# A state-space block on one core: one wait of VectorE for four exponentials made 8 units ahead, aggregates and scales a slot behind their sources, delta projections in two pairs

## The chip, the core and the metric

The kernel runs on one core of a Trainium2 chip. The metric is the device time of one execution in microseconds. The five engines of the core that matter are TensorE (PE: matmuls, and transposes as matmuls), VectorE (DVE), ScalarE (ACT), GpSimd (POOL) and SyncE (SP, which issues most of the DMAs). Each runs its own list of instructions in order; an instruction waits for semaphores that others raise, and everything behind it on its engine waits with it.

## What is computed

The input `x` is 8 sequences of 2048 tokens with 512 channels, float32. The block is a selective state-space layer (S6) with a residual, and then a feed-forward layer with quantized weights and a residual:

```python
u = layernorm(x)
xp = u @ x_proj_w.T                     # 512 -> 64 (rank) + 16 (B) + 16 (C)
delta = softplus(xp[..., :64] @ dt_proj_w.T + dt_proj_b)
h = exp(delta * A) * h + delta * B * u  # over time, for each channel and each of 16 states
y = (h * C).sum(states) + u * D
x = x + y
z = layernorm(x)                        # z quantized to int8 by row, times int8 weights
x = x + (round(z / s) @ weight_q.T) * s * weight_scale + bias
```

The recurrence over time is the heart: 16 states x 512 channels, each a scan along the sequence.

## The kernel before

**Tiling.** The sequence is cut into chunks of 512 tokens: four to a sequence, 32 in all. Within a chunk the recurrence is cut into 64 *units*: 16 states `n` times four groups `d` of 128 channels. A unit is one scan of VectorE over a tile of 128 channels x 512 tokens. The main loop takes one *slot* for each unit, so a chunk has slots 0 to 63, and unit u = 4n + d is scanned in slot u. The loop only writes instructions into the engines' lists; there is no barrier between slots, and each engine runs ahead as far as its waits and buffers allow. All instructions of the loop are pinned to the order in which they are written (`pin`), so the order written by hand is each engine's order.

**What a slot writes**, in this order (main loop, lines 552 to 573):

- in the first slot of a state: `c_mult` of the state before (GpSimd: the last column of h into `state[n]`, line 485, then h times C over all four groups at once, line 488), and every second state a load of two rows of C (SP, line 476)
- `exp_unit`, ScalarE, line 412: exp(delta x A) of a unit some places ahead, into a tile `da`. The counter `ahead` starts at 5; slots 28 to 31 make none, and slots 21, 23, 25 and 33 make two. There are 8 `da` buffers, each free again when its scan is done
- `bt_piece`, ScalarE, line 428: a quarter of B x delta x u of the state two ahead (`bT`). For states 1, 5, 9 and 13 this is one DMA instead (a diagonal of B, `dg`), so slots 28 to 31 have no such ScalarE work
- `b_pe`, TensorE: turns B x delta x u of the unit two ahead into channel-major order in one of three PSUM banks (`pb`; line 451 by four transposes, line 442 by products with the diagonal)
- `scan`, VectorE, line 460: h of the unit from `da`, `pb` and the state carried over. In the first chunk of a sequence the carried state is the constant 0
- `y_pe`, TensorE, line 513: adds h x C of the unit ten back into the output y (`hc` transposed back)
- then the steps that `todo` holds for this slot: pieces of `prep` (the first layer norm and the projections of the next chunk) and of `post` (residual, second layer norm and the feed-forward of the chunk before)

**The steps of `prep` and `post`.** Each list gives a slot to every step; where two share a slot, `post` comes first. In `prep`: the statistics of the input are taken one chunk earlier still, in slots 21 to 27 (`stats`: bn_stats and bn_aggr on VectorE, lines 148 and 149), the reciprocal root on GpSimd (`rstd_of`), normalization (line 173), transposes of the normalized input (14 to 21), the projection to 96 rows (`xp_pe`, slots 22 and 23), its copy (`xp_act`, slot 24, line 207), the transpose of B (`bt_pe`, 25; `bt_act`, 26, which also sends four small DMAs), then delta: `dt_pe` (27 to 30, TensorE, line 247) and `softplus` (28 to 31, ScalarE, line 257), one group of channels in each slot, and last delta x u: `dlt_pe` (TensorE, line 265) and `du` (VectorE, line 270), slots 38 to 45. Softplus and exp lie in different tables of ScalarE: a table load stands before the first softplus and before the first exponential after the last.

In `post`: loads of the input (`load`, slots 1 to 4, SP, line 297), `residual` (7, 8, 10, 12; VectorE, line 301), `stats` (14, 16, 18, 19), normalization (31 to 34; line 306, into z), `amax` (33, 34, 36, 37: a reduction and at once the scale `xs` from it, lines 324 and 330), the reciprocal of the scales (38), rounding (40 to 43), and for each of four token tiles transposes of z (`q_pe`), their copy to bf16 (`q_act`), the product with the weights (`o_pe`, line 371) and its scaling (`o_out`: VectorE, line 380; GpSimd adds the residual, line 384; SP stores, line 385). GpSimd adds the bias to the residual in slots 35, 39, 43 and 47 (line 317).

**One bank for all of these.** Every TensorE result of `prep` and `post` (`misc`) goes through one PSUM bank; each must be read before the next is written.

Of the kernel before, what the change touches and what calls it, by code (L numbers as in the profile page):

```python
# [17 lines left out]
P = 128  # L18
# [8 lines left out]
def kernel(  # L27
# [112 lines left out]
    cts, bcs = {}, {}  # L140
    mvs, nmrs, rstds, x1, zs, qts = {}, {}, {}, {}, {}, {}
    das, pbs, bts, hs, hcs, ys = {}, {}, {}, {}, {}, {}

    def stats(key, i, n, src):
        if i == 0:
            mvs[key] = small.tile([P, n, 2], F32, tag=f"mv{n}", name=f"mv_{key}")
        st = small.tile([P, 6], F32, tag="st", name=f"st_{key}_{i}")
        pin(nc.vector.bn_stats(st, src))  # L148
        pin(nc.vector.bn_aggr(mvs[key][:, i, :], st))
# [16 lines left out]
    def prep(k):  # L166
# [106 lines left out]
        for i in range(NT):  # L273

            steps.append((21 + 2 * i - SLOTS, lambda i=i: stats(key, i, NT, xn[k][:, i, :])))
            steps.append((5 + i, lambda i=i: norm(i)))
            steps.append((14 + 2 * i, lambda i=i: xnt_pe(i)))
            steps.append((15 + 2 * i, lambda i=i: xnt_act(i)))
            steps.append((22 + i // 2, lambda i=i: xp_pe(i)))
            steps.append((27 + i, lambda i=i: dt_pe(i)))  # L280
            steps.append((28 + i, lambda i=i: softplus(i)))
            steps.append((38 + 2 * i, lambda i=i: dlt_pe(i)))
            steps.append((39 + 2 * i, lambda i=i: du(i)))
        steps.append((27 - SLOTS, lambda: rstd_of(key, NT)))
        steps.append((24, xp_act))
        steps.append((25, bt_pe))
        steps.append((26, bt_act))
        return sorted(steps, key=lambda at: at[0])

    def post(k):  # L290
# [28 lines left out]
        def amax(i):  # L319
            if i == 0:  # L320
                st["am"] = small.tile([P, NT], F32, tag="am", name=f"am_{k}")
                st["xs"] = small.tile([P, NT], F32, tag="xs", name=f"xs_{k}")
            pin(
                nc.vector.tensor_reduce(
                    st["am"][:, i : i + 1], zs[i], AX.X, ALU.max, apply_absolute_value=True
                )
            )

            pin(
                nc.vector.tensor_scalar(  # L330
                    st["xs"][:, i : i + 1],
                    st["am"][:, i : i + 1],
                    Q_EPS,
                    1.0 / 127.0,
                    ALU.max,
                    ALU.mult,
                )
            )
# [49 lines left out]
        for i in range(NT):  # L388
            steps.append((1 + i, lambda i=i: load(i)))
            steps.append(((7, 8, 10, 12)[i], lambda i=i: residual(i)))  # L390
            steps.append(((14, 16, 18, 19)[i], lambda i=i: stats(key, i, NT, x1[k, i])))
            steps.append((31 + i, lambda i=i: norm(i)))
            steps.append(((33, 34, 36, 37)[i], lambda i=i: amax(i)))
            steps.append((35 + 4 * i, lambda i=i: add_bias(i)))
            steps.append((40 + i, lambda i=i: rnd(i)))
            steps.append(((46, 48, 52, 56)[i], lambda i=i: q_pe(i)))
            steps.append(((47, 49, 53, 57)[i], lambda i=i: q_act(i)))
            steps.append(((50, 54, 58, 60)[i], lambda i=i: o_pe(i)))
            steps.append(((51, 55, 59, 61)[i], lambda i=i: o_out(i)))
        steps.append((19, lambda: rstd_of(key, NT)))  # L400
        steps.append((38, scales))
# [4 lines left out]
    def exp_unit(u):  # L406
# [4 lines left out]
        t = work.tile([P, T], F32, tag="da", bufs=8, name=f"da_{k}_{n}_{d}")  # L411
        pin(nc.scalar.activation(t, delta[k][:, d, :], AF.Exp, scale=a_neg[:, d, n : n + 1]))  # L412
        das[u] = t
# [40 lines left out]
    def scan(u):  # L454
        s, d = divmod(u, ND)
        k, n = divmod(s, N)
        if d == 0:
            hs[s] = work.tile([P, ND, T], F32, tag="h", bufs=3, name=f"h_{k}_{n}")
        pin(
            nc.vector.tensor_tensor_scan(  # L460
                hs[s][:, d, :],
                das.pop(u),
# [5 lines left out]
        )  # L468

# [73 lines left out]
    ahead = 5  # L543
# [8 lines left out]
    for k in range(NCHUNK + 1):  # L552
        for slot in range(SLOTS):
# [6 lines left out]
            if slot < 28 or slot > 31:  # L560

                for _ in range(2 if slot in (21, 23, 25, 33) else 1):
# [59 lines left out]
```

## Time and profile before

The median of three runs is 3148.9 us (3147.22 to 3153.0).

| | |
|---|---|
| profiled execution, its own time | 3150.26 us |
| its span | 3148.5 us |
| VectorE busy | 2931.5 us, 93% |
| TensorE busy (matmuls) | 2864.0 us, 91% |
| GpSimd busy | 2798.1 us, 89% |
| ScalarE busy | 2795.1 us, 89% |
| scans (lines 460) | 2048, 1261 ns with a state and 1201 ns without |
| exponentials (line 412) | 2048, 715 ns |
| h x C (line 488) | 512, 4566 ns |
| DMA | 276.78 MB, 88 GB/s |
| granted TensorE clock | 0.989 |

A busy time is the sum of the instructions' lengths as recorded. On VectorE and ScalarE the next instruction starts some 0.08 to 0.1 us before the recorded end of the one before, so the distance from start to start is the better measure of what an instruction costs: ten scans that are recorded with 1.25 us each take 11.7 us. A wait is shown in brackets as the idle time before an instruction and the instruction that ended it. Where an instruction waits for several engines, all but one of its waits are instructions of their own ahead of it, which the views do not count as busy.

### The profile page before, as it was taken

To read this page: it belongs to the slowest core of one execution; us is meant where nothing else is said; L and a number is where in the kernel's file an instruction comes from. 1 tells how busy PE (TensorE), PEld (TensorE's weight loads), DVE (VectorE), ACT (ScalarE), POOL (GpSimd) and SP (SyncE) were. 2 spreads that over 40 slices of the span, in tenths; PEclk is the share of its full clock that TensorE was granted. 3 is DMA by queue.
4 is the path that set the end of the run, shared out by engine and by line. 5 is a ranking of instruction groups with operands and counts; after the bars stand their busy time and mean duration, and the time that the engine had idled before them with its cause. 6 is when DMAs were issued, how large, how long until landed. Compare 5 with 4: busy or idle time off the path is not lost.

```text
span 3148.5 us, 58120 instructions
## 1 busy us (share of the span) xinstructions
PE 2864.0 (91%) x22050; PEld 2465.4 (78%) x22144; DVE 2931.5 (93%) x3239; ACT 2795.1 (89%) x4482; POOL 2798.1 (89%) x1417
## 2 busy tenths in 40 slices
PE   5999999999999999999999999999999999999996
PEld 4877888777887778887878877878878788877784
DVE  4999999999999999999999999999999999999995
ACT  5998899988999989899888999988999889998883
POOL 2889899988999889999898998999999998998896
PEclk8999999999999999999999999999999999999997
DMA  4222323223223123332233232233232232322221
GB/s 122 89 59 91 102 88 101 79 70 103 94 95 102 55 89 101 98 98 86 64 95 102 88 101 60 86 98 98 98 95 62 89 101 88 101 81 70 87 88 41
DMA packets 182105, 276.78 MB, mean 88 GB/s; under 512 B 81152, under 2 KB 81664, under 8 KB 181824
## 3 DMA queue, kind: packets, MB, share of 16 engines
q1 hardware_dynamic: 177664, 269.80, 27.3%
q8 instruction: 175, 2.87, 0.4%
q10 hardware_dynamic: 4160, 3.25, 0.3%
q14 instruction: 106, 0.87, 0.1%
HBM read 236.03 MB, written 36.96 MB: 87 GB/s over the span
## 4 chain that ended last, share of the span: by engine, by line
PE 40%; ACT 23%; DVE 15%; POOL 11%; issue 9%; DMA 1%; SPq 0%; ACTq 0%; POOLq 0%; DVEq 0%
PE y L513 11%; DVE h L460 11%; PE pb L451 9%; ACT da L412 9%; POOL hc L488 8%; ACT bT L428 7%; PE pb L442 7%; PE y L501 4%; PE pdt L247 3%; PE po L371 2%; ACT z L348 2%; DVE st_a L148 1%; PE pz L354 1%; PE pxp L197 1%; PE pxn L185 1%
## 5 line engine op out<-in xcount | busy, mean ns | idle before, releaser
L488 POOL TENSOR_TENSOR hc<-h,c 128x2048 f32<-128x2048 f32 x512 | 2335.7, 4566 | 30.3 <-issue 12.7
L460 DVE TENSOR_TENSOR_SCAN h<-da,state,pb 128x512 f32<-128x512 f32 x1536 | 1864.8, 1261 | 52.6 <-PE pb L451 52.1
L412 ACT ACTIVATE da<-delta,a_neg 128x512 f32<-128x512 f32 x2048 | 1423.5, 715 | 32.1 <-DVE h L460 31.6
L513 PE MATMUL y<-ident,hc 128*128 128x128 f32 x8192 | 1231.2, 273 | 5.6 <-POOL hc L488 5.6
L428 ACT ACTIVATE bT<-x,BT 128x512 f32<-128x512 f32 x1536 | 1093.6, 712 | 4.8 <-DVE x L270 4.8
L451 PE MATMUL pb<-ident,bT 128*128 128x128 f32 x6144 | 957.5, 278 | 133.1 <-DVE h L460 109.4
L451 PEld LDWEIGHTS pb<-ident,bT 128*128 128x128 f32 x6144 | 700.7, 141 | 387.7 <-issue 136.7
L513 PEld LDWEIGHTS y<-ident,hc 128*128 128x128 f32 x8192 | 965.4, 142 | 6.2 <-POOL hc L488 6.2
L460 DVE TENSOR_TENSOR_SCAN h<-da,pb 128x512 f32<-128x512 f32 x512 | 591.8, 1201 | 28.2 <-PE pb L451 24.8
L442 PE MATMUL pb<-dg,x 128*128 128x128 f32 x4096 | 561.1, 280 | 40.2 <-DVE h L460 38.0
L442 PEld LDWEIGHTS pb<-dg,x 128*128 128x128 f32 x4096 | 500.6, 192 | 80.7 <-DVE h L460 72.3
L384 POOL TENSOR_TENSOR o<-o,x 128x512 f32<-128x512 f32 x128 | 164.5, 1285 | 52.2 <-DVE o L380 48.9
L247 PE MATMUL pdt<-xp,dtproj_sb 128*128 128x512 f32 x256 | 144.1, 645 | 48.6 <-ACT delta L257 40.8
L190 ACT COPY xnT<-pxn 128x512 f32<-128x512 f32 x128 | 73.6, 575 | 119.4 <-PE pxn L185 119.4
L257 ACT ACTIVATE delta<-pdt,dtb_sb 128x512 f32<-128x512 f32 x128 | 88.2, 689 | 96.1 <-PE pdt L247 95.7
L317 POOL TENSOR_TENSOR x<-x,bias_b 128x512 f32<-128x512 f32 x128 | 163.7, 1280 | 0.9 <-ACT z L306 0.9
L380 DVE SCALAR_TENSOR_TENSOR o<-po,xs,ws_b 128x512 f32<-128x512 f32 x128 | 94.5, 738 | 52.6 <-PE po L371 52.6
L485 POOL COPY state<-h 128x4 f32<-128x4 f32 x384 | 75.2, 196 | 75.8 <-DVE h L460 70.7
L501 PE MATMUL y<-diag_d,xnT 128*128 128x128 f32 x1024 | 137.8, 278 | 0.0
L371 PE MATMUL po<-wq_sb,qT 128*128 128x512 bf16 x418 | 129.6, 388 | 8.7 <-ACT qT L360 2.2
L501 PEld LDWEIGHTS y<-diag_d,xnT 128*128 128x128 f32 x1024 | 127.0, 195 | 0.0
L306 ACT ACTIVATE z<-x,nmr_f,rstd_f 128x512 f32<-128x512 f32 x128 | 102.2, 801 | 24.9 <-POOL nmr_f L160 24.9
(51 smaller groups left out, 1685.5 us busy)
## 6 DMA issues: line engine op xcount, KB each, us to landing
c<-bc SPq DMA_DIRECT2D x256, 512.0 KB, 4.0
x<-in_x_dram SPq DMA_DIRECT2D x32, 1024.0 KB, 7.5
dg<-dg SPq DMA_DIRECT2D x128, 256.0 KB, 4.1
x<-in_x_dram SPq DMA_DIRECT2D x128, 256.0 KB, 6.1
out_dram<-o SPq DMA_DIRECT2D x128, 256.0 KB, 2.0
dg<-zeros ACTq DMA_DIRECT2D x8, 256.0 KB, 3.1
dg<-BT SPq DMA_DIRECT2D x128, 2.0 KB, 3.2
bc<-xp SPq DMA_DIRECT2D x32, 32.0 KB, 1.6
```

The source lines that it names most:

```text
L247: nc.tensor.matmul(pd, lhsT=dtproj_sb[:, ts(d, P)], rhs=xp, start=True, stop=True)
L317: pin(nc.gpsimd.tensor_tensor(x1[k, i], x1[k, i], bias_b, ALU.add))
L371: nc.tensor.matmul(po, lhsT=qt[:, d, :], rhs=wq_sb[:, d, :], start=(d == 0), stop=(d == ND - 1))
L384: pin(nc.gpsimd.tensor_tensor(o, o, x1.pop((k, i)), ALU.add))
L412: pin(nc.scalar.activation(t, delta[k][:, d, :], AF.Exp, scale=a_neg[:, d, n : n + 1]))
L428: nc.scalar.activation(bts[s][:, i, :], xn[k][:, i, :], AF.Copy, scale=b_t[k][:, i, n : n + 1])
L442: nc.tensor.matmul(pb[:, ts(i, P)], lhsT=xn[k][:, i, ts(d, P)], rhs=bts[s][:, i, :], start=True, stop=True,)
L451: pin(nc.tensor.transpose(pb[:, ts(i, P)], bts[s][:, i, ts(d, P)], ident))
L460: nc.vector.tensor_tensor_scan(hs[s][:, d, :], das.pop(u), pbs.pop(u), 0.0 if k % CPB == 0 else state[n][:, d : d + 1], ALU.mult, ALU.add,)
L488: pin(nc.gpsimd.tensor_tensor(hc, h, c.unsqueeze(1).to_broadcast([P, ND, T]), ALU.mult))
L501: nc.tensor.matmul(y[:, ts(d, P)], lhsT=xn_t[k, d][:, ts(i, P)], rhs=diag_d[:, d, :], start=(d == 0), stop=False, skip_group_check=True,)
L513: nc.tensor.matmul(y[:, ts(d, P)], lhsT=hcs[s][:, d, ts(i, P)], rhs=ident, is_transpose=True, start=False, stop=(n == N - 1 and d == ND - ...
```

## The change

Six things, all in the order of the instructions and in their waits; no operation of the computation is added or taken away.

1. Exponentials are made 8 units ahead instead of 5, with 10 `da` buffers instead of 8. Slots 27 to 31 make none (before: 28 to 31), and slots 33, 35, 37, 39 and 41 make two (before: 21, 23, 25 and 33).
2. The scan of a state's first group of channels gets a dependency on the exponential of its fourth group, so that it waits for all four exponentials of the state; the other three scans then have nothing of ScalarE left to wait for.
3. bn_aggr is a step of its own one slot behind its bn_stats, for both layer norms, and the GpSimd step that reads the aggregates moves by one slot. Likewise the scale `xs` stands a slot behind its `amax`.
4. The transpose of B and its copy come a slot earlier (24, 25). The delta projections stand in slots 26, 27, 29 and 30 with softplus in 27, 28, 30 and 31: two pairs, with a slot between. delta x u moves from slots 38 to 45 to slots 33 to 40.
5. amax moves to slots 35, 37, 39 and 41, the scales' reciprocal to 42, rounding to 43 to 46.
6. The steps of the feed-forward product: transposes of z in 44, 46, 51, 56 (copies a slot later), products in 48, 53, 58, 61, their scaling in 50, 55, 60, 63.

```diff
+    def aggregate(key, i):
+        pin(nc.vector.bn_aggr(mvs[key][:, i, :], sts.pop((key, i))))
...
             steps.append((21 + 2 * i - SLOTS, lambda i=i: stats(key, i, NT, xn[k][:, i, :])))
+            steps.append((22 + 2 * i - SLOTS, lambda i=i: aggregate(key, i)))
...
-            steps.append((27 + i, lambda i=i: dt_pe(i)))
-            steps.append((28 + i, lambda i=i: softplus(i)))
-            steps.append((38 + 2 * i, lambda i=i: dlt_pe(i)))
-            steps.append((39 + 2 * i, lambda i=i: du(i)))
-        steps.append((27 - SLOTS, lambda: rstd_of(key, NT)))
+            steps.append(((26, 27, 29, 30)[i], lambda i=i: dt_pe(i)))
+            steps.append(((27, 28, 30, 31)[i], lambda i=i: softplus(i)))
+            steps.append((33 + 2 * i, lambda i=i: dlt_pe(i)))
+            steps.append((34 + 2 * i, lambda i=i: du(i)))
+        steps.append((28 - SLOTS, lambda: rstd_of(key, NT)))
         steps.append((24, xp_act))
-        steps.append((25, bt_pe))
-        steps.append((26, bt_act))
+        steps.append((24, bt_pe))
+        steps.append((25, bt_act))
...
+            steps.append(((15, 17, 19, 20)[i], lambda i=i: aggregate(key, i)))
             steps.append((31 + i, lambda i=i: norm(i)))
-            steps.append(((33, 34, 36, 37)[i], lambda i=i: amax(i)))
+            steps.append((35 + 2 * i, lambda i=i: amax(i)))
+            steps.append((36 + 2 * i, lambda i=i: scale(i)))
             steps.append((35 + 4 * i, lambda i=i: add_bias(i)))
-            steps.append((40 + i, lambda i=i: rnd(i)))
-            steps.append(((46, 48, 52, 56)[i], lambda i=i: q_pe(i)))
-            steps.append(((47, 49, 53, 57)[i], lambda i=i: q_act(i)))
-            steps.append(((50, 54, 58, 60)[i], lambda i=i: o_pe(i)))
-            steps.append(((51, 55, 59, 61)[i], lambda i=i: o_out(i)))
-        steps.append((19, lambda: rstd_of(key, NT)))
-        steps.append((38, scales))
+            steps.append((43 + i, lambda i=i: rnd(i)))
+            steps.append(((44, 46, 51, 56)[i], lambda i=i: q_pe(i)))
+            steps.append(((45, 47, 52, 57)[i], lambda i=i: q_act(i)))
+            steps.append(((48, 53, 58, 61)[i], lambda i=i: o_pe(i)))
+            steps.append(((50, 55, 60, 63)[i], lambda i=i: o_out(i)))
+        steps.append((20, lambda: rstd_of(key, NT)))
+        steps.append((42, scales))
...
-        t = work.tile([P, T], F32, tag="da", bufs=8, name=f"da_{k}_{n}_{d}")
+        t = work.tile([P, T], F32, tag="da", bufs=10, name=f"da_{k}_{n}_{d}")
...
+        if d == 0:
+            tc.add_manual_dep(
+                ins.ins,
+                das[u + ND - 1][1].ins.name,
+                mybir.DependencyInfo(mybir.DependencyClass.Sync, mybir.DependencyReason.DATA),
+                reason="all four exponentials",
+            )
...
-    ahead = 5
+    ahead = 8
...
-            if slot < 28 or slot > 31:
-                for _ in range(2 if slot in (21, 23, 25, 33) else 1):
+            if slot < 27 or slot > 31:
+                for _ in range(2 if slot in (33, 35, 37, 39, 41) else 1):
```

More of the change, by code (lines that the diff above doesn't have):

```diff
@@ L140 @@
     cts, bcs = {}, {}
+    sts = {}
     mvs, nmrs, rstds, x1, zs, qts = {}, {}, {}, {}, {}, {}
@@ L148, in stats @@
         pin(nc.vector.bn_stats(st, src))
-        pin(nc.vector.bn_aggr(mvs[key][:, i, :], st))
+        sts[key, i] = st
+    def aggregate(key, i):
+        pin(nc.vector.bn_aggr(mvs[key][:, i, :], sts.pop((key, i))))
     def rstd_of(key, n):
@@ L327, in amax, with scale @@
             )
+        def scale(i):
             pin(
@@ L410, in exp_unit @@
         k, n = divmod(s, N)
-        t = work.tile([P, T], F32, tag="da", bufs=8, name=f"da_{k}_{n}_{d}")
-        pin(nc.scalar.activation(t, delta[k][:, d, :], AF.Exp, scale=a_neg[:, d, n : n + 1]))
-        das[u] = t
+        t = work.tile([P, T], F32, tag="da", bufs=10, name=f"da_{k}_{n}_{d}")
+        das[u] = t, pin(
+            nc.scalar.activation(t, delta[k][:, d, :], AF.Exp, scale=a_neg[:, d, n : n + 1])
+        )
     def bt_piece(s, i):
@@ L458, in scan @@
             hs[s] = work.tile([P, ND, T], F32, tag="h", bufs=3, name=f"h_{k}_{n}")
-        pin(
+        ins = pin(
             nc.vector.tensor_tensor_scan(
                 hs[s][:, d, :],
-                das.pop(u),
+                das[u][0],
                 pbs.pop(u),
@@ L468, in scan @@
         )
+        if d == 0:
[4 more added lines that the diff above has]
+                reason="all four exponentials",
+            )
+        del das[u]
     def load_c(s):
```

## The prediction

> **What bounds the kernel now.** I read the page's busy shares first (VectorE 93%, TensorE 91%, ScalarE and GpSimd 89%: four engines close together, so shares decide nothing), then the timeline of VectorE over one chunk (the one from 1002.70 to 1098.89 us), then those of the other engines at the places where VectorE stood still. Columns: start, length, engine, line, operation, and the idle time before it with what ended it. VectorE:
>
> ```profile
> 1044.42 3.62 DVE L460 TENSOR_TENSOR_SCAN h<-da,state,pb 128x512 f32<-128x512 f32 x3
> 1048.94 1.28 DVE L460 TENSOR_TENSOR_SCAN h<-da,state,pb 128x512 f32<-128x512 f32 x1 [0.90 <-PE pb L451]
> 1050.87 1.28 DVE L460 TENSOR_TENSOR_SCAN h<-da,state,pb 128x512 f32<-128x512 f32 x1 [0.65 <-PE pb L451]
> 1052.75 1.28 DVE L460 TENSOR_TENSOR_SCAN h<-da,state,pb 128x512 f32<-128x512 f32 x1 [0.60 <-PE pb L451]
> ...
> 1081.35 0.75 DVE L380 SCALAR_TENSOR_TENSOR o<-po,xs,ws_b 128x512 f32<-128x512 f32 x1 [0.21 <-PE po L371]
> ...
> 1087.51 0.75 DVE L380 SCALAR_TENSOR_TENSOR o<-po,xs,ws_b 128x512 f32<-128x512 f32 x1 [0.71 <-PE po L371]
> ...
> 1096.53 11.81 DVE L460 TENSOR_TENSOR_SCAN h<-da,state,pb 128x512 f32<-128x512 f32 x10
> ```
>
> See two things. Ten scans without a stall take 11.73 us from start to start (1096.53 to 1108.26), 1.17 each, whatever they wait for: VectorE is the pace of most of the chunk. And it loses time in two places: slots 31 to 34, where each scan waits for its B x u product (`pb`) or an amax for its z, and the two `o` products of slots 51 and 55. Taking each start-to-start time against the shortest of its kind, the chunk's 96.19 us hold 90.3 of work and 5.9 of loss: 3.15 in slots 31 to 34 (0.98, 0.76, 0.84, 0.57), 1.08 at slots 51 and 55 (0.29, 0.79), and about 1.6 in small pieces. In the first chunk of a sequence (no state operand, 94.0 us) these are 3.7 and 2.24. The chunks repeat to 0.01 us.
>
> ScalarE in the same stretch, and TensorE just before it:
>
> ```profile
> 1039.90 0.58 ACT L207 COPY xp<-pxp 96x512 f32<-96x512 f32 x1 [1.12 <-PE pxp L197]
> ...
> 1045.24 1.28 ACT L257 ACT_TABLE_LOAD   x1
> 1046.53 0.69 ACT L257 ACTIVATE delta<-pdt,dtb_sb 128x512 f32<-128x512 f32 x1
> 1048.43 0.69 ACT L257 ACTIVATE delta<-pdt,dtb_sb 128x512 f32<-128x512 f32 x1 [1.22 <-PE pdt L247]
> ...
> 1052.24 0.69 ACT L257 ACTIVATE delta<-pdt,dtb_sb 128x512 f32<-128x512 f32 x1 [0.52 <-PE pdt L247]
> 1052.95 1.28 ACT L412 ACT_TABLE_LOAD   x1
> 1054.25 0.72 ACT L412 ACTIVATE da<-delta,a_neg 128x512 f32<-128x512 f32 x1
> ```
>
> ```profile
> 1034.52 0.60 PE L451 MATMUL pb<-ident,bT 128*128 128x128 f32 x4
> 1034.96 0.60 PE L513 MATMUL y<-ident,hc 128*128 128x128 f32 x4
> 1035.40 1.88 PE L197 MATMUL pxp<-xnT,xproj_sb 128*96 128x512 f32 x4
> ```
>
> From 1045.24 to 1054.25 ScalarE makes no exponential. VectorE scans on regardless: at slot 32 it needs only exponential 32, finished long before (those of slots 32 to 35 were 10 to 12 us old). Call the `pb` at 1034.52 (slot 22) P; all offsets below are from P. It stands 0.40 behind the end of scan 21. Before: xp copy P+5.38, first softplus P+12.01, scan 32 P+16.35, scan 36 P+23.78 (23.39 in the first chunk of a sequence).
>
> **What the Trainium skill says.** "VectorE: DVE Perf Modes", section "The DRAIN you can't avoid", finds that semaphores between VectorE operations cost nothing extra. The trace agrees: 1.17 a scan with one wait or two. The same section says a same-engine read after a write needs a semaphore or another operation between; the trace shows the price, bn_stats to bn_aggr 0.70 where other 512-wide operations are followed after 0.58. "ScalarE: Activation LUTs", section "What ACT_TABLE_LOAD costs", gives 1283 ns and a drain, 2.66 us a switch. The trace shows the 1.28 but the softplus 0.01 behind it; I use 1.30.
>
> **The change, part by part.**
>
> *Waits of the scans.* Three of four scans lose a wait on ScalarE. Cover: they run 1.17 apart already; gain 0. The first scan of a state now waits for exponential u+3. Exponentials run 8 ahead, so this is covered by five slots, except after slots 27 to 31, where five are left out: then the last one made is 34, and exponential 35 is issued in slot 32 itself, behind the four softplus and the second table load. Scan 32 waits for it. Queued behind that scan on VectorE are scans 33 to 35, du and amax; GpSimd and TensorE then run dry too.
>
> *When exponential 35 is done.* TensorE spacings from the trace: pb 0.44, y 0.44, xp pair 1.72 with its lead 0.44, pdt 0.96, before a pdt 0.51. From P: slots 22 and 23 with the xp pairs, then pb 26 P+5.18, y 5.62. The transpose of B follows in slot 24 (waits for the xp copy, ends 5.96) at 6.12; pb 27 6.45, pb 28 7.33, y 7.76, first pdt 8.27 to 9.40. ScalarE, from the xp copy at 5.38: copy 0.48, exponential 0.62, bT 0.62, B copy 0.10, exponential 0.62, two bT 0.62 and 0.72, table load 1.30: first softplus 10.45 to 11.14. One bank serves all pdt, so the second pdt starts at 11.19. pb 30 12.15, y 12.59, slot 29: pb 31 13.03, y 13.46, third pdt 13.97, pb 32 14.93, fourth pdt 15.88 to 17.0. Fourth softplus 17.04 to 17.73, table load to 19.03, exponential 35 to 19.76. Scan 32 starts at P+19.85 (before: 16.35). VectorE would have been there at about P+15.2: scan 30 waits 1.2 for its pb, then it stands 4.65.
>
> *Then.* ScalarE has to pass bT, z, two exponentials, bT, z, exponential, bT, z before exponential 39: 6.42 us of measured starts plus 0.71, P+26.17. VectorE's own work from scan 32 is four scans, one du, one amax, 5.87, P+25.7: scan 36 starts at P+26.25. Against before +2.48 in a chunk with state, +2.86 in the first of a sequence. The a-statistics' saved time (four pairs in slots 21 to 28) lies in this stretch and is worth nothing; so is the saving on GpSimd, which no longer waits for the aggregate ahead of a product. Exponential 43 is done 4 us before scan 40.
>
> *Aggregates of the f-statistics* (slots 14 to 20, before P): bn_stats and bn_aggr take 0.80 together, apart 0.58 + 0.10; four a chunk with the late starts behind them, -0.54. TensorE has four diagonal-B slots there (1.4 each) and lags a little more at P: +0.15 (0 to 0.3).
>
> *Slots 36 to 46*: amax and scale apart save 0.13 twice; the reciprocal now reads a scale just written, +0.12; two of the four du move in. -0.05.
>
> *Output products.* o_pe leads each o_out by two slots instead of one. TensorE ends po 0.6 us or more before VectorE comes: the loss at 51 and 55 goes, -1.08 and -2.24.
>
> *The tail of the chunk on GpSimd and SP.* GpSimd takes 4.66 us a product and 5.88 with an `o` add. o_out 2 and 3 move to slots 60 and 63, so both adds stand behind the product of slot 60; VectorE, 1.1 faster there, leaves GpSimd further behind. SP is in order: the last store, a C load and then the x1 loads.
>
> ```profile
> 1101.42 0.33 SPq L385 DMA_DIRECT2D out_dram<-o  x1
> 1101.81 0.42 SPq L476 DMA_DIRECT2D c<-bc  x1
> 1102.28 0.91 SPq L297 DMA_DIRECT2D x<-in_x_dram  x2
> ```
>
> The store stood 2.53 behind the chunk's start (1098.89); now GpSimd ends its add at about +3.65 (+4.8 after a chunk without state). x1 loads land 4.4 to 5 after issue, so at about +9.4 (+10.5); the residual of slot 7 comes at +9.37. y of the last state is about as late. Cost 0.15, after a stateless chunk 1.0 (0 to 1.5).
>
> *Start.* The first scan waits for four exponentials instead of one, with 0.61 each: +1.5 to +1.8, taken 1.5.
>
> *Sum*, against the profiled execution's own 3150.26 us (span 3148.5; 1.4 above the median of the runs):
> stage of slots 22 to 36: 23 x 2.48 + 7 x 2.86 + 2.5 for the first chunk = +79.5; lag +4.7; f-aggregates -16.7; slots 36 to 46 -1.5; output products 24 x 1.08 + 7 x 2.24 = -41.6; x1 24 x 0.15 + 7 x 1.0 = +10.6; start +1.5. Together +36.5: 3186.8, as a median 3185.
>
> **Rivals.** *Faster: the wait of slot 32 is hidden.* If the chain from the xp copy to exponential 35 is shorter than I add it, each 1 us is worth 31 us; from 1.2 us on (a stall at slot 32 under 3.5 us) the gains at the aggregates and output products win. Two us shorter gives 3123. For it: ScalarE has three exponentials fewer in slots 21 to 25 and ten buffers, and the pairs move the first softplus 1.5 us forward (P+10.45 for 12.01). Against: exponential 35 can't come before the fourth softplus, and that needs pdt 4, four slots after pdt 1 on a TensorE that lags. 12%.
> *A draw*: the chain 1 to 1.3 us shorter, or x1 never late and lag nil together with 0.7 us less chain: about 3150. 8%.
> *The transfers decide as well*: x1 and y late by 1 us in every chunk instead of 0.15 adds 20 to 30: 3212. The thin margin before (a landing 0.09 to 1.1 us ahead of its residual) speaks for it, the free SP queue against. 8%.
> *The waits don't go* (the scans keep theirs): nothing changes, since they cost nothing.
>
> **How the numbers follow.** Main case 72%, own range 3160 to 3208. With the rivals: faster by over 0.2% 12%, within 0.2% 8%, slower 80% (0.2% is about what a measurement of this kernel tells from no change). The range 3146 to 3212 leaves out the faster case and the upper half of the transfers' case, and a little of the main one's edges.
>
> **What would show it.** Right: one stall of 4 to 5 us a chunk at scan 32, put down to ScalarE's `da`; the three `pb` stalls shrunk to one of about 1; no stall before the `o` products; bn_stats followed by a scan after 0.58; chunk period about 97.2 (before 96.19). Wrong, if scan 32 waits under 3.5 us, if the fourth softplus starts before P+16.5, or if VectorE stalls at the residuals by more than 1 us in each chunk.

## The result, and the profile after

The changed kernel takes 3190.27 us in the median of four runs (3186.83 to 3197.87), the kernel before 3150.14 (3147.22 to 3153.0, with one run more than in the section on the kernel before): 1.0131 of the time before, 95% interval 1.011 to 1.0151. The profiled execution took 3186.83 us, with a span of 3184.9 (before 3150.26 and 3148.5). It is slower by 1.3%, and the predicted 3185 lies five us below the median.

The scan is line 469 now, the exponential 421, bT 437, the transposed `pb` 460 and the one with the diagonal 451, y 531, softplus 261, `pdt` 251, amax 329, the output scaling 386, its add on GpSimd 390 and its store 391, the x1 load 302, the residual 306.

First VectorE, the timeline of the changed kernel in the chunk from 1017.37 us; P, the `pb` of slot 22, is at 1049.01. Columns as before: start, length, engine, line, operation, and in brackets the idle time ahead and what ended it.

```profile
1059.50 1.24 DVE L469 TENSOR_TENSOR_SCAN h<-da,state,pb 128x512 f32<-128x512 f32 x1
1061.81 2.45 DVE L469 TENSOR_TENSOR_SCAN h<-da,state,pb 128x512 f32<-128x512 f32 x2 [1.07 <-PE pb L460]
1068.70 3.62 DVE L469 TENSOR_TENSOR_SCAN h<-da,state,pb 128x512 f32<-128x512 f32 x3 [4.44 <-ACT da L421]
...
1075.11 1.28 DVE L469 TENSOR_TENSOR_SCAN h<-da,state,pb 128x512 f32<-128x512 f32 x1 [0.44 <-issue]
...
1096.72 0.72 DVE L386 SCALAR_TENSOR_TENSOR o<-po,xs,ws_b 128x512 f32<-128x512 f32 x1
1103.23 0.72 DVE L386 SCALAR_TENSOR_TENSOR o<-po,xs,ws_b 128x512 f32<-128x512 f32 x1
```

The three `pb` stalls of slots 31 to 33 and the wait of slot 34 for an amax are gone; one `pb` stall stands at slot 30 (1.07), and then VectorE stands 4.44 us at scan 32, put down to the exponential. Scan 36 (1075.11) waits another 0.44; the view calls that "issue", and it ends 0.09 behind the end of exponential 39 (P+26.00). The `o` products of slots 50 and 55 have no stall ahead of them.

ScalarE in the same stretch, from the copy of xp on:

```profile
1054.39 0.58 ACT L211 COPY xp<-pxp 96x512 f32<-96x512 f32 x1 [1.73 <-PE pxp L201]
1054.88 0.72 ACT L421 ACTIVATE da<-delta,a_neg 128x512 f32<-128x512 f32 x1
...
1058.18 1.28 ACT L261 ACT_TABLE_LOAD   x1
1059.47 0.69 ACT L261 ACTIVATE delta<-pdt,dtb_sb 128x512 f32<-128x512 f32 x1
...
1063.98 0.69 ACT L261 ACTIVATE delta<-pdt,dtb_sb 128x512 f32<-128x512 f32 x1 [1.92 <-PE pdt L251]
1064.57 0.80 ACT L311 ACTIVATE z<-x,nmr_f,rstd_f 128x512 f32<-128x512 f32 x1
1065.89 0.69 ACT L261 ACTIVATE delta<-pdt,dtb_sb 128x512 f32<-128x512 f32 x1 [0.52 <-PE pdt L251]
1066.60 1.28 ACT L421 ACT_TABLE_LOAD   x1
1067.89 0.72 ACT L421 ACTIVATE da<-delta,a_neg 128x512 f32<-128x512 f32 x1
```

The first softplus is at P+10.46, the fourth at P+16.88, and the exponential for unit 35 starts behind the table load at P+18.88. Scan 32 follows 0.09 behind its end.

How VectorE's waits add up over the whole execution, in the view of waits (who waits for whom, us in total, times, longest). Before:

```profile
DVE h L460 <- PE pb L451: 76.9, 99, 2.2
DVE o L380 <- PE po L371: 52.6, 66, 6.9
```

And after:

```profile
DVE h L469 <- ACT da L421: 139.9, 32, 4.6
DVE h L469 <- PE pb L460: 45.7, 43, 1.9
DVE o L386 <- PE po L377: 16.2, 4, 6.4
```

Of the 32 waits for `da`, 31 are those of scan 32, one in each chunk but the last, and one is the start; together they take 139.9 us. The waits for `pb` and `po` shrank by 67.6.

To see where gains and losses lie, I took the starts of scans 0, 14, 22, 36 and 47 of each chunk in the profiled executions and summed the difference to before, in us, over 30 chunks (the second to the 31st). All the runs stand in the table, so that it serves below; what each kernel is follows under the experiments. The *make-up* is the doubled slots in which ScalarE makes the exponentials that were left out; *own waits* means that each scan waits for its own exponential alone.

| kernel (median, ratio to before) | slots 0-14 | 14-22 | 22-36 | 36-47 | 47-64 |
|---|---|---|---|---|---|
| the change (3190, 1.0131) | +16.9 | -24.1 | +81.2 | +0.4 | -39.8 |
| own waits (3176, 1.0080) | 0.0 | -25.3 | -34.4 | +68.3 | +17.7 |
| exponential 35 first (3158, 1.0021) | +7.6 | -24.7 | +40.9 | +0.4 | -19.8 |
| early loads (3167, 1.0056) | 0.0 | -25.4 | +80.3 | +0.5 | -40.0 |
| delta projections in one row (3193, 1.0129) | +19.2 | -24.6 | +81.0 | +0.4 | -39.8 |
| one wait, late make-up (3228, 1.0244) | +7.4 | -24.7 | +114.7 | +0.4 | -25.5 |
| own waits, late make-up (3109, 0.9872) | +5.5 | -24.6 | -1.7 | +0.5 | -18.9 |
| own waits, make-up in slots 1 to 12, early loads (3067, 0.9736) | -3.2 | -25.3 | -34.4 | +0.6 | -18.7 |
| before + one wait (3185, 1.0112) | +2.1 | -1.0 | +37.8 | +0.8 | -5.3 |
| before + aggregates (3124, 0.9915) | +2.0 | -25.3 | -3.4 | -3.3 | +4.9 |
| before + output steps (3249, 1.0315) | -0.4 | +0.3 | +0.3 | +109.2 | -10.1 |
| before + output steps and du (3152, 1.0006) | +24.9 | +2.9 | +18.4 | -18.0 | -20.6 |
| the same with early loads (3126, 0.9923) | -0.7 | 0.0 | +18.0 | -18.0 | -20.6 |

In the last two rows du, moved ahead, takes 18 us from the fourth column to the third (in the change amax moves the other way and evens that out). In the first row, 0.22 us a chunk of the second column comes back in the third: the aggregate of slot 21 now stands in slot 22, while P hangs on scan 21.

### The profile page after: what moved, and what is told of

It reads as the page before. It is cut to its first block, busy times and chain, and to the rows that moved or that the text cites. A ratio compares the mean times of both kernels' runs of the same rounds, so it can differ in the third digit from the quotient of the medians.

```text
span 3184.9 us, 58015 instructions
## 1 busy us (share of the span) xinstructions
PE 2824.6 (89%) x22144; PEld 2485.8 (78%) x22144; DVE 2887.5 (91%) x3239; ACT 2799.1 (88%) x4482; POOL 2797.8 (88%) x1417
## 4 chain that ended last, share of the span: by engine, by line
PE 41%; DVE 28%; ACT 16%; issue 7%; DMA 3%; POOL 3%; SPq 0%; ACTq 0%; POOLq 0%; DVEq 0%
DVE h L469 22%; PE y L531 11%; PE pb L460 9%; PE pb L451 7%; ACT da L421 6%; ACT bT L437 4%; PE pxp L201 3%; PE y L519 3%; PE pdt L251 3%; DMA x<-in_x_dram 3%; PE po L377 2%; DVE am L329 2%; ACT z L311 2%; DVE x L274 2%; POOL hc L506 2%
## 5 line engine op out<-in xcount | busy, mean ns | idle before, releaser
L421 ACT ACTIVATE da<-delta,a_neg 128x512 f32<-128x512 f32 x2048 | 1434.8, 714 | 69.8 <-DVE h L469 67.6
L460 PE MATMUL pb<-ident,bT 128*128 128x128 f32 x6144 | 948.0, 277 | 249.3 <-DVE h L469 172.5
L451 PEld LDWEIGHTS pb<-dg,x 128*128 128x128 f32 x4096 | 513.8, 197 | 30.7 <-DVE h L469 20.9
L390 POOL TENSOR_TENSOR o<-o,x 128x512 f32<-128x512 f32 x128 | 162.7, 1283 | 13.9 <-DVE o L386 10.6
L251 PE MATMUL pdt<-xp,dtproj_sb 128*128 128x512 f32 x256 | 137.7, 620 | 38.4 <-ACT delta L261 38.1
L201 PE MATMUL pxp<-xnT,xproj_sb 128*96 128x512 f32 x256 | 122.1, 600 | 0.7 <-ACT xnT L194 0.7
```

The source lines that it names most:

```text
L201: nc.tensor.matmul(st["pp"][:E], lhsT=xproj_sb[:, d, :], rhs=xn_t[k, d], start=(d == 0), stop=(d == ND - 1),)
L251: nc.tensor.matmul(pd, lhsT=dtproj_sb[:, ts(d, P)], rhs=xp, start=True, stop=True)
L451: nc.tensor.matmul(pb[:, ts(i, P)], lhsT=xn[k][:, i, ts(d, P)], rhs=bts[s][:, i, :], start=True, stop=True,)
L460: pin(nc.tensor.transpose(pb[:, ts(i, P)], bts[s][:, i, ts(d, P)], ident))
```

## Experiments

The theory that the runs had to test: the change is slower because the joint wait (that of a state's first scan for all four exponentials) makes scans 32 and 36 wait for exponentials 35 and 39, which the left-out slots 27 to 31 and the table loads make late; without that the rest is a gain. Rivals: the make-up or the pairs of projections are what costs, whichever wait the scan has; or the gains that I counted on aren't there.

### The wait alone, taken away and added

Own waits: the changed kernel without the joint dependency.

```diff
-        if d == 0:
-            tc.add_manual_dep(
-                ins.ins,
-                das[u + ND - 1][1].ins.name,
...
```

> The changed kernel without the joint wait: each scan waits for its own exponential, all slots as changed. Offsets from P, the pb of slot 22. My theory (the loss is scan 32 being held for exponential 35): scan 32 starts when its pb is there, about P+15.6 (changed kernel 19.69), scans 33 and 34 when theirs are (17.5, 18.7), delta x u at 20.2, scan 35 at 20.7 with its exponential just in time (19.7), scan 36 at about 22.5 (26.09): 3.6 us a chunk less, 3190 - 31 x 3.6 = about 3078, faster than before. Rival (the exponentials are late whoever waits for them, because five slots make none and ScalarE is behind): VectorE meets the late ones one by one at 35 to 39, exponential 39 ends at P+26.0 as now and scan 36 moves by 1 us at most: 3160 to 3190.

Measured: 3175.84 us, 1.0080 (1.0063 to 1.0097). Scan 32 starts at P+15.50 and scan 36 at P+22.30, as expected, and slots 22 to 36 give back 115.6 us against the change. The total falls by 14 only. The 3.8 us by which VectorE leads at scan 36 are lost again at slots 47 to 55. The timeline of TensorE in this kernel shows where (P of the chunk at 1045.07):

```profile
1080.92 0.65 PE L460 MATMUL pb<-ident,bT 128*128 128x128 f32 x4 [0.35 <-DVE h L469]
1081.41 0.60 PE L523 MATMUL y<-ident,hc 128*128 128x128 f32 x4
1084.62 0.66 PE L360 MATMUL pz<-ident,z 128*128 128x128 f32 x4 [2.60 <-ACT z L354]
1085.11 0.60 PE L460 MATMUL pb<-ident,bT 128*128 128x128 f32 x4
```

and that of ScalarE shows what it waited for, with no idle time ahead of any instruction:

```profile
1083.24 0.71 ACT L437 ACTIVATE bT<-x,BT 128x512 f32<-128x512 f32 x1
1083.86 0.70 ACT L354 ACTIVATE z<-z,rs 128x512 f32<-128x512 f32 x1
```

The first transposes of z (`q_pe`, slot 44) wait 2.60 for ScalarE's rounding (line 354), and the `pb` products that VectorE scans next stand behind them on TensorE. ScalarE is not waiting there: its list between slots 32 and 47 is the usual one plus the five exponentials of the make-up, 0.61 each, and the rounding comes at P+38.8. In the changed kernel this is hidden, because VectorE reaches scan 46 only at P+41.84; here it is there at P+38.05. So the joint wait covers a second bound, and taking it away uncovers that. My expectation of 3078 fell, on the sum and not on the stage it was worked out for. A part of the loss is TensorE at half its clock behind that wait (last section).

Before + one wait: the old order with the dependency alone.

```diff
+        if d == 0:
+            tc.add_manual_dep(
+                ins.ins,
+                das[u + ND - 1][1].ins.name,
...
```

> The kernel before with the joint wait alone (5 ahead, 8 buffers, all slots as before). Theory: three waits fewer on a state's scans gain nothing, as scans already follow each other after 1.17 us. Scan 32 needs exponential 35, made in slot 27, no loss. Scan 36 needs exponential 39, which ends at P+24.9 where the scan stood at P+23.78: 1.2 to 1.3 us a chunk, and 1.5 at the start: 3150 + 40 = 3190. Rival (a wait taken away is worth something, 10 to 25 ns a scan, 48 scans a chunk): 0.5 to 1.2 us a chunk back, 3150 to 3175.

Measured: 3185.38, 1.0112 (1.0097 to 1.0127). Five ahead, with slots 28 to 31 left out, exponential 35 is made before the pause, so scan 32 stays at P+16.38 (16.35), but scan 36 waits for exponential 39. The timeline of ScalarE in this kernel (P at 1047.41) has exponential 39 at:

```profile
1071.64 0.71 ACT L413 ACTIVATE da<-delta,a_neg 128x512 f32<-128x512 f32 x1
```

and that of VectorE scan 36 at:

```profile
1072.44 1.28 DVE L461 TENSOR_TENSOR_SCAN h<-da,state,pb 128x512 f32<-128x512 f32 x1 [1.15 <-POOL state L495]
```

The bracket names GpSimd, but the wait ends 0.09 behind the end of exponential 39 (1072.35); the dependency was the only edit. Scan 36 moves from P+23.77 to 25.03, which is the +37.8 of the table. Everything else is nearly unchanged (no other column moves by more than 5.3), the 48 scans a chunk that lose their wait on ScalarE among it: the removed waits are worth nothing that can be seen.

### Exponential 35 before the pause

```diff
-            if slot < 27 or slot > 31:
-                for _ in range(2 if slot in (33, 35, 37, 39, 41) else 1):
+            if slot < 28 or slot > 31:
+                for _ in range(2 if slot in (33, 35, 37, 39) else 1):
```

> The changed kernel with slot 27 making its exponential (35) again, so that it stands ahead of the first table load; slots 28 to 31 make none, and 33, 35, 37 and 39 make two. The joint wait stays. My theory: softplus and all behind it are 0.62 us later (first at P+11.1), scan 32 no longer waits for ScalarE and starts at about P+16; scan 36 now waits for exponential 39, which ends at about P+24.7: scan 36 at 24.8 for 26.09, 1.3 us a chunk less: about 3150, level with before. Rival (the loss is spread over TensorE and transfers): no change, 3185 to 3195.

Measured: 3157.96, 1.0021 (1.001 to 1.0032). Scan 32 is at P+16.12 instead of 19.68, but scan 36 only at 24.77 instead of 26.09, because it then waits for exponential 39. Taking 3.6 us from the chain of scan 32 is worth 40 us in slots 22 to 36 (1.3 a chunk), and half of that goes at once: the gain of slots 47 to 64 falls from 39.8 to 19.8.

### The place of the made-up exponentials

Late make-up, with and without the joint wait: four ahead, and the doubles in slots 19 to 25 and 33 instead of 33 to 41 (the same edit is made to the change, for the run with the wait, and to own waits, for the run without).

```diff
-    ahead = 8
+    ahead = 4
...
-                for _ in range(2 if slot in (33, 35, 37, 39, 41) else 1):
+                for _ in range(2 if slot in (19, 21, 23, 25, 33) else 1):
```

> The changed kernel without the joint wait, and with the five left-out exponentials made up in slots 33, 19, 21, 23 and 25 (the last four in the next chunk, the counter starts at 4) instead of 33 to 41. New theory: the change holds VectorE by two bounds that run side by side, the joint wait at scan 32 and ScalarE's list of slots 32 to 47, where five made-up exponentials push the rounding of z (slot 43) 2.5 us back; taking the wait alone away let VectorE run into the second at slots 47 to 50. With both gone scan 36 stays at P+22.3, the rounding stands at about P+36.3 instead of 38.8, the stalls at 47 to 50 shrink from 3.3 us to under 1, and the chunk loses about 3.5 us instead of 7.7: 3190 - 31 x 3.9 = about 3065. Rival (ScalarE's sum of work over the chunk is the bound, wherever it lies): the made-up exponentials in slots 19 to 25 hold up the transposed copies and the xp copy, 3140 to 3180.

> The changed kernel with its joint wait, and with the exponentials made up in slots 33, 19, 21, 23 and 25 (counter from 4). New theory: up to exponential 39 ScalarE's list is the same, so scan 32 still starts at P+19.7 and scan 36 at P+26.1; VectorE is then later than ScalarE's list anyway and gains nothing: 3180 to 3195. Rival (the made-up exponentials alone are the loss, not the wait): about 100 us less, near 3090.

Measured: own waits 3109.33, 0.9872 (0.9856 to 0.9889), between the two expectations; one wait 3227.56, 1.0244 (1.0229 to 1.0259), above both. In slots 36 to 47 the 68.3 us of the kernel with own waits are down to 0.5: with four of the five doubles moved out of slots 33 to 41 the rounding comes at P+37.3 in the mean instead of 38.8, VectorE reaches scan 46 at P+39.0, and the stalls at 47 to 50 are gone. So it was the place of the make-up that uncovered the second bound. What I had not seen is a price at the new place. The double of slot 25 stands between the copy of xp and the first softplus, and the projection ahead of that copy is late too. The timelines of TensorE and ScalarE in the kernel with one wait (P at 1060.44):

```profile
1061.68 1.96 PE L201 MATMUL pxp<-xnT,xproj_sb 128*96 128x512 f32 x4 [0.20 <-ACT xnT L194]
...
1066.26 0.58 ACT L211 COPY xp<-pxp 96x512 f32<-96x512 f32 x1 [0.34 <-PE pxp L201]
1066.74 1.34 ACT L421 ACTIVATE da<-delta,a_neg 128x512 f32<-128x512 f32 x2
1067.98 0.71 ACT L437 ACTIVATE bT<-x,BT 128x512 f32<-128x512 f32 x1
```

P itself is not later against scan 21 in chunks with state (1.55 us behind its start here and in the change), but the projection starts at P+1.24 instead of 0.88, because it waits for ScalarE's last copy of the transposed input, and the copy of xp at P+5.82 instead of 5.38. Behind it stand two exponentials where the change has one. In the mean of the chunks with state the first softplus is at P+11.5 instead of 10.5, scan 32 (one wait) at P+20.7 instead of 19.7, scan 36 (own waits) at 23.3 instead of 22.3. The table puts it at 1.1 us a chunk, 33.5 us with one wait (114.7 against 81.2) and at 32.7 with own waits (-1.7 against -34.4). The two runs also fix the price of the joint wait in slots 22 to 36: 115.6 us with the early make-up, 116.4 with the late one. It doesn't depend on the place of the make-up. The rest of the miss with one wait lies in slots 47 to 64, where the gain is 14 us smaller (0.22 at slot 48, 0.36 at slot 60). In each of the 30 chunks scans 48 and 60 start 0.09 behind the end of exponentials 51 and 63, for which the joint wait holds them: in this order these are late.

Own waits, make-up in slots 1, 3, 10, 12 and 33, early loads:

```diff
-    ahead = 8
+    ahead = 4
...
-                for _ in range(2 if slot in (33, 35, 37, 39, 41) else 1):
+                for _ in range(2 if slot in (1, 3, 10, 12, 33) else 1):
...
-            steps.append((1 + i, lambda i=i: load(i)))
+            steps.append((i - 8, lambda i=i: load(i)))
```

and without the dependency, as above.

> The changed kernel with own waits, x1 loads in slots 56 to 59 of the chunk before, and the exponentials made up in slots 33, 1, 3, 10 and 12 (counter from 4). Theory: in the run with 19, 21, 23 and 25 the double slot 25 put one more exponential between the xp copy and the first softplus (P+11.15 for 10.46, scan 36 at 23.0 for 22.3) and 19 and 21 let TensorE lag at P by 0.35 more; in slots 1 to 12 ScalarE has room. First softplus back at P+10.46, scan 36 at 22.3, the residuals not held: 1.1 to 1.3 us a chunk below that run's 3109: 3070 (3062 to 3082). Rival (slots 1 to 12 have no room, or VectorE meets TensorE in slots 47 to 55 as before): 3100 to 3115.

Measured: 3067.22, 0.9736 (0.9722 to 0.9751), as expected, and better than both kernels: 2.6% below before. The timeline of VectorE in this kernel, slots 30 to 34 of one chunk:

```profile
1023.49 2.45 DVE L469 TENSOR_TENSOR_SCAN h<-da,state,pb 128x512 f32<-128x512 f32 x2 [1.13 <-PE pb L460]
1026.13 1.28 DVE L469 TENSOR_TENSOR_SCAN h<-da,state,pb 128x512 f32<-128x512 f32 x1 [0.18 <-POOL nmr_a L164]
1028.01 2.45 DVE L469 TENSOR_TENSOR_SCAN h<-da,state,pb 128x512 f32<-128x512 f32 x2 [0.60 <-PE pb L460]
```

The stall of slot 30 is that of the change (1.13 for 1.07); behind it the scans follow with 0.18 and 0.60 instead of 4.44. A chunk with state takes 93.44 us (before 96.18).

### The loads

The changed kernel with the x1 loads issued in slots 56 to 59 of the chunk before.

```diff
-            steps.append((1 + i, lambda i=i: load(i)))
+            steps.append((i - 8, lambda i=i: load(i)))
```

> The changed kernel with the four loads of x1 in slots 56 to 59 of the chunk before instead of 1 to 4, ahead of the two last stores on SP. Theory: the residuals of slots 7 and 10 wait for these loads (0.60 and 0.10 us a chunk on the mean); with the loads early that goes, unless y of the last state is as late: 12 to 22 us less, 3168 to 3178. Rival (y is as late as the load): no change within 5 us.

Measured: 3167.17, 1.0056 (1.0041 to 1.0071), 23 us below the change. Slots 0 to 14 fall from +16.9 to 0.0 and no other column moves by more than 1.3. In the changed kernel the timeline of GpSimd around the start of a chunk (1114.57 us) is this:

```profile
1111.12 4.56 POOL L506 TENSOR_TENSOR hc<-h,c 128x2048 f32<-128x2048 f32 x1
1115.62 2.54 POOL L390 TENSOR_TENSOR o<-o,x 128x512 f32<-128x512 f32 x2
```

and that of SP, which issues the transfers:

```profile
1116.95 1.57 SPq L391 DMA_DIRECT2D out_dram<-o  x2
1118.57 0.42 SPq L494 DMA_DIRECT2D c<-bc  x1
1119.05 0.92 SPq L302 DMA_DIRECT2D x<-in_x_dram  x2
```

Both adds stand behind the product, the stores behind the adds, the loads behind the stores: issued 4.48 behind the start (before 3.4), landing at +9.2 to 11.0 in chunks with state. The residual of slot 7, for which VectorE is ready at +9.37, follows 0.09 behind the landing. That is the step as predicted; it cost 0 to 1.7 us from chunk to chunk, 0.58 in the mean of those with state.

### The pairs

The changed kernel with the projections in slots 26 to 29 and softplus in 27 to 30, without the empty slot.

```diff
-            steps.append(((26, 27, 29, 30)[i], lambda i=i: dt_pe(i)))
-            steps.append(((27, 28, 30, 31)[i], lambda i=i: softplus(i)))
+            steps.append((26 + i, lambda i=i: dt_pe(i)))
+            steps.append((27 + i, lambda i=i: softplus(i)))
```

> The changed kernel with delta's projections in slots 26 to 29 and softplus in 27 to 30, one row instead of two pairs; joint wait and the rest as changed. Theory: the empty slot between the pairs puts one pb and one y (0.87 us) between the second and the third projection, and exponential 35, for which scan 32 waits, hangs on the fourth: scan 32 at P+18.8 for 19.7, scan 36 at 25.2 for 26.1: 0.87 x 31 = 27 us less, 3163 (3158 to 3170). Rival (without the slot VectorE runs out of pb, and the wait only moves): no change.

Measured: 3192.51, 1.0129 (1.0113 to 1.0144): no difference to the change, where I expected 27 us. The timeline of ScalarE in this kernel:

```profile
1062.31 0.69 ACT L261 ACTIVATE delta<-pdt,dtb_sb 128x512 f32<-128x512 f32 x1 [1.22 <-PE pdt L251]
1062.89 0.81 ACT L311 ACTIVATE z<-x,nmr_f,rstd_f 128x512 f32<-128x512 f32 x1
1063.72 1.28 ACT L421 ACT_TABLE_LOAD   x1
1065.02 0.72 ACT L421 ACTIVATE da<-delta,a_neg 128x512 f32<-128x512 f32 x1
```

The fourth softplus is 0.70 earlier (P+16.17), but the normalization of slot 31, which in the change fills the gap ahead of the fourth softplus, now stands between it and the table load, which starts 1.41 behind that softplus instead of 0.71. Scan 32 starts at P+19.68 in both. So the pairs cost nothing here. As the rival had it, a part of the wait only moves: 0.74 us a chunk now stand at scan 31, for its `pb`. But what holds scan 32 is exponential 35, as before.

### The aggregates and the output steps by themselves

Before + aggregates: bn_aggr and the scale a slot behind, in the old order.

```diff
+            steps.append((22 + 2 * i - SLOTS, lambda i=i: aggregate(key, i)))
...
+            steps.append(((15, 17, 19, 20)[i], lambda i=i: aggregate(key, i)))
+            steps.append(((34, 35, 37, 38)[i], lambda i=i: scale(i)))
```

> The kernel before with the aggregates and the scales a slot behind their sources, and nothing else. Theory: 0.54 us a chunk from the four pairs of slots 14 to 20 and 0.2 to 0.26 from the scales of slots 36 to 38; nothing from the four pairs of slots 21 to 28, because slots 31 to 34 wait for a chain of TensorE and ScalarE that starts at P: 0.75 x 31 = 23 us less, 3127. Rival (each pair is worth its 0.13 wherever it stands): 1.35 x 31 = 42 us less, 3108.

Measured: 3123.56, 0.9915 (0.99 to 0.993), as the theory had it and not the rival. Slots 14 to 22 give 25.3 us, as in every kernel that has this edit. The a-statistics' pairs give next to nothing (-3.4 in slots 22 to 36): the stall of slot 31 grows from 1.06 to 1.44, that of slot 51 from 0.54 to 0.71.

Before + output steps: transposes, products and scalings of the feed-forward at their new slots, nothing else.

```diff
-            steps.append(((46, 48, 52, 56)[i], lambda i=i: q_pe(i)))
...
+            steps.append(((44, 46, 51, 56)[i], lambda i=i: q_pe(i)))
+            steps.append(((45, 47, 52, 57)[i], lambda i=i: q_act(i)))
+            steps.append(((48, 53, 58, 61)[i], lambda i=i: o_pe(i)))
+            steps.append(((50, 55, 60, 63)[i], lambda i=i: o_out(i)))
```

> The kernel before with the steps q_pe, q_act, o_pe and o_out in the slots of the change, and nothing else. Theory: the stalls ahead of the output products go (1.08 us a chunk, 2.24 in the first of a sequence, 42 us in all), and the later last stores bring the x1 loads of the next chunk up to their residuals, 0.3 to 0.6 us a chunk, 10 to 18 us: 3150 - 28 = 3122 (3115 to 3130). Rival (the loads are not late): 3108.

Measured: 3249.0, 1.0315 (1.0299 to 1.033), a miss by 127 us. The view of waits of this kernel:

```profile
DVE x L270 <- PE pdl L265: 135.8, 33, 28.2
PEld pdl L265 <- ACT qT L360: 126.4, 30, 4.6
```

All of these results go through one PSUM bank. The last delta x u transposes (`pdl`, slot 44) stand behind the first transposes of z, now in slot 44 too, wait for their copy in slot 45, and VectorE's du of slot 45 waits with them:

```profile
1100.22 2.44 DVE L460 TENSOR_TENSOR_SCAN h<-da,state,pb 128x512 f32<-128x512 f32 x2
1106.30 0.69 DVE L270 TENSOR_TENSOR x<-pdl,x 128x512 f32<-128x512 f32 x1 [3.64 <-PE pdl L265]
```

So the two moves belong together: du has to leave slots 38 to 45 first. Two more runs did that, on the kernel before: output steps and du, and the same with the loads in slots 56 to 59 of the chunk before.

```diff
-            steps.append((38 + 2 * i, lambda i=i: dlt_pe(i)))
-            steps.append((39 + 2 * i, lambda i=i: du(i)))
+            steps.append((33 + 2 * i, lambda i=i: dlt_pe(i)))
+            steps.append((34 + 2 * i, lambda i=i: du(i)))
```

> The kernel before with q_pe, q_act, o_pe and o_out in the slots of the change, and with delta x u moved to slots 33 to 40 as in the change, and nothing else. In the run with the four output steps alone the transposes of z (slot 44) took the one bank ahead of the last transposes of delta (slot 44 too), and VectorE's du of slot 45 stood 3.3 to 4.4 us for them. Theory: that stall goes, the stalls of slots 51 and 55 are 1.4 us a chunk less, TensorE's diagonal slots 50 to 53 keep 0.7 at 54 and 55, the loads of x1 cost 0.1 to 0.3: 10 to 25 us less than before, 3125 to 3140. Rival (the output steps cost VectorE time wherever du stands): over 3160.

> The kernel before with the output steps in the slots of the change, delta x u in slots 33 to 40, and the loads of x1 in slots 56 to 59 of the chunk before. In the run without the early loads the stalls of slots 51 and 55 were gone (1.4 us a chunk on the mean), and 0.65 at slot 7, 0.1 at slot 10 and 0.2 at slots 14 and 16 had come, with 0.57 at slots 54 and 55. Theory: the late loads of x1 ate the gain of the output steps; with them early 0.75 to 0.95 us a chunk come back: 3152 - 26 = 3126 (3120 to 3132). Rival (y of the last state is as late as the loads, or the gain was lost elsewhere): 3145 to 3153.

Measured: 3152.11, 1.0006 (0.9997 to 1.0015), and with early loads 3125.79, 0.9923 (0.9906 to 0.9941). Slots 47 to 64 give 20.6 us in both; in the first of them slots 0 to 14 take 24.9 back, in the second nothing. The view of waits of the first has this line, and that of the second has none for the load:

```profile
DVE x L301 <- DMA x<-in_x_dram: 16.5, 24, 2.1
```

With the loads out of the way the output steps are a gain of 0.8%. But it is half of what I had given them: both stalls before the `o` products are gone here, and new ones of 0.30 and 0.27 a chunk stand at slots 54 and 55. In the change the gain is 39.8; I read the difference as TensorE coming forward while VectorE stands 4.5 us at scan 32. That is argued and not shown: what speaks for it is that the gain is 18.7 to 20.6 in every kernel here with these slots and without a long stall there (but for own waits with the early make-up, whose stalls lie in these very slots).

## Why the prediction was right

Point by point, by its own steps.

**The wait of scan 32.** Right, to 0.2 us. The first softplus was forecast at P+10.45 and came at 10.46, exponential 35's end 19.76 and 19.60, scan 32 19.85 and 19.68, its stall 4.65 and 4.52, that of scan 30 1.2 and 1.14, exponential 39's end 26.17 and 26.00, scan 36 26.25 and 26.09. The fourth softplus came at 16.88 where 17.04 was worked out. The stage was forecast at +2.48 a chunk and measured at +2.31 (+2.71 for +2.86 without state). That the wait causes it is shown: without the dependency the stage falls by 115.6 us. It is not all that makes the kernel slow: without the wait it is still 0.8% slower than before, without it and with the late make-up 1.3% faster, and the late make-up with the wait is 2.4% slower. The prediction had the first of these two bounds and not the second.

**Nothing for the removed waits, nothing for the a-statistics.** Right: adding the joint wait to the kernel before left all other scans nearly where they were, and the aggregates alone gave nearly all they gave in slots 14 to 22.

**Aggregates of the f-statistics, -16.7.** Right: of the -24.1, 0.22 a chunk comes back later, which leaves -17.5. A bn_stats is followed after 0.58 now; the aggregate by itself takes 0.07 to the next start, less than the 0.10 that I used.

**Lag at P, +0.15 a chunk.** Wrong in chunks with state: P mostly stands 0.35 behind the end of scan 21 (before 0.40). Only in chunks without state it comes later than before, by 0.26 in most. Summed over the 30 chunks that is +1.6 instead of +4.7.

**Slots 36 to 46, -1.5.** +0.4: of no weight.

**Output products, -41.6.** Measured -39.8, right in size and in part for another reason. I had said that the two slots of lead alone take these stalls away. The runs show half: 20.6 us by themselves, 18.7 to 19.8 wherever the stall at scan 32 is short or absent. The other half was seen only with that stall; why is argued and not shown. With 3.6 us less of it (exponential 35 first), half the gain was gone.

**x1 loads, +10.6.** The mechanism right, the size off: slots 0 to 14 cost 16.9, and moving the loads gave 23. The mis-sized term is mainly the 0.15 of 23 of these chunks: they lose 0.38 at the residual of slot 7, and the seven behind a chunk without state 1.19 where 1.0 was reckoned. The 0.15 came from one landing time, about +9.4, with "4.4 to 5" us from issue to landing. The trace before has 4.4 to 6.7 for the first load of a chunk, and its chunks do not all "repeat to 0.01 us": seven of the 23 with state take longer than 96.20, up to 97.54, and most of these have a late residual at slot 7. Only lateness costs, so such a spread costs more than its mean would.

**Start, +1.5.** Measured +2.4; the first chunk cost +0.8 where 2.5 was reckoned, and the last is 2.8 shorter.

The misses (+6 at the loads, -7 at the stage and the lag together, +4 at the small terms, -3 at the first and last chunk) nearly cancel; that the sum met the profiled time to 0.1 us is luck at that precision.

**The faster rival** was wrong as it was worked out, though it never came to be tried by the change itself: "each 1 us is worth 31 us", and a chain two us shorter would give 3123. The experiments that shortened it show two other bounds behind. Exponential 39 stops scan 36 (3.6 us less at scan 32 was worth 1.3 a chunk), and with no wait at all ScalarE's rounding, delayed by the make-up in slots 33 to 41, stops the `pb` products at slot 47: 3176, where the same arithmetic gives about 3078. The prediction costed the make-up only where it delays exponential 39; the rounding behind it in the same list does not occur in it. It took both edits, own waits and the make-up elsewhere, to get the gain.

## What to carry to other kernels

A wait for the last of a group costs what the last one is late; look for the pause in the producer's list (here five left-out slots and two table loads) and count from its end, not in units of lead. A bunch of made-up work delays all that stands behind it in the same list, and a large stall can hide that: before a stall's removal is priced, ask what each engine would have ready at the earlier time. Steps that share one bank or one queue may not bear being moved one by one, as the output steps without du showed, and the cost of a thin margin is the mean of the late cases, not the lateness of the mean.

## What had not been expected of the hardware

**An idle time of 2.4 us was enough to halve TensorE's clock.** In the kernel with own waits, TensorE waits 2.6 us for the rounding in nearly every chunk with state and 3.15 in those without; in 18 of the 23 and in all 7 it runs at half speed around that place. Its timeline, in a chunk where that happened, behind the same wait as shown above:

```profile
698.17 1.11 PE L360 MATMUL pz<-ident,z 128*128 128x128 f32 x4 [2.59 <-ACT z L354]
699.08 1.06 PE L460 MATMUL pb<-ident,bT 128*128 128x128 f32 x4
```

The four `pb` transposes take 0.85 us to the next start instead of 0.44. The granted clock by windows of this kernel (window, length, busy time and count of PE, PEld, DVE, ACT and POOL, then PEclk, DMA share and GB/s), first this chunk, then the one shown earlier:

```profile
698.00:704.00 6.00, 5.83 (x28) 5.83 (x29) 2.56 (x2) 5.30 (x10) 4.81 (x4) 0.50 0.02 3
...
1084.50:1090.00 5.50, 4.85 (x41) 4.49 (x42) 4.18 (x4) 5.50 (x11) 5.18 (x4) 1.00 0.00 0
```

In the clock record of each execution, away from its first and last 75 us, such stretches last 3.4 or 6.8 us: 1 in the kernel before, 19 in the change (17 of them around the 2.4 us for which TensorE waits for scan 32), 25 with own waits, 30 with the output steps alone (where TensorE waits 3.8 to 4.4 us), none in the fastest kernel. The Trainium skill, "TensorE: Matmul & The Clock Gate", section "Part 1: The HAM clock gate (the "warmup" mystery)", says that the clock is halved after an idle window of about 3.4 us of a counter that runs freely. That the stretches last 3.4 and 6.8, and that the same wait does it in some chunks only, agrees with that. That idle times of 2.4 and 2.6 us, less than a window, were enough here does not. In the change it costs next to nothing: from scan 22 to the end of the chunk those with state take 65.42 us with such a stretch and 65.37 without. With own waits it does: from scan 36 to the end they take 43.6 us with it (18 chunks) and 42.4 without (5 chunks). By an estimate from these two means, if chunks without state lose as much, 25 chunks of it are some 30 us, a good part of what this kernel gave back behind scan 36.

**The price of a read behind a write on VectorE has two halves.** With a scan between, a bn_stats is followed after 0.58 instead of 0.70, and the aggregate itself is also shorter: recorded 0.16 instead of 0.18 in the mean, and 0.07 instead of 0.10 to the next start (from the timeline: 1039.58 to 1039.65 in the changed kernel). The amax and its scale, now apart, show the same (0.58 for 0.69, 0.04 for 0.07), and the reciprocal, which now stands directly behind the last scale that it reads, starts 0.16 behind it.
